# Cross-attention and a routed feed-forward on one core: turning activations through memory and VectorE's blocks instead of on TensorE, and writing the empty rows two at a time

## The chip, the cores and the metric

The kernel runs on one core of one Trainium2 chip. A core has TensorE (matmuls, in profiles PE, and its weight loads PEld), VectorE (DVE), ScalarE (ACT), GpSimd (POOL) and SyncE (SP), which run their own instruction streams and wait for each other through semaphores; 16 DMA engines move data between the device's memory, called DRAM in the code, and the core's SBUF. The metric is device time in microseconds for one execution. All data are 32-bit floats.

## The reference

Eight batches of 256 rows of 512 numbers are normalised, attend to a context, are added back, are normalised again, and go through a shared and a routed feed-forward layer.

```python
# x, ctx: (8, 256, 512)
def xattn(q, k, v):                      # 32 heads of 16, 8 groups of keys and values
    qh, kh, vh = heads(q @ Wq.T), heads(k @ Wk.T), heads(v @ Wv.T)
    attn = softmax(qh @ kh.T / sqrt(16))
    return (attn @ vh) @ Wfc.T + bfc

def ffn(h):                              # 8 experts, 352 wide; each row goes to 2
    scores = softmax(h @ gate_weight.T)  # 4 groups of 2; the 2 best groups count
    wmat = top2_within_best_groups(scores)
    routed = sum_n wmat[:, n] * ((silu(h @ gate_w[n].T) * (h @ up_w[n].T)) @ down_w[n].T)
    shared = (silu(h @ sh_gate_w.T) * (h @ sh_up_w.T)) @ sh_down_w.T   # 704 wide
    return routed + shared

x = x + xattn(layernorm(x), ctx, ctx)
x = x + ffn(layernorm(x))
```

## The kernel before

The contraction of a matmul runs over the 128 partitions, so an activation tile of 128 rows by 512 columns has to be turned before its columns can be contracted. The kernel does this in two places of the attention phase. In `project(b)` (L894) the normalised input rows of batch b are turned into `xT` and multiplied with `wq_sb` (L921). In `close(b)` (L1035), which multiplies the attention's result with `wfc_sb`, adds the residual into `acc` and normalises it, the normalised rows `lnf` are turned into `hT`; `hT` feeds the router's product (L1094) and the shared layer's first products (L181, `Shared.pieces`). Both use `transposed` (L822): four TensorE transposes of 128 x 128 into PSUM, and one copy into SBUF by ACT or VectorE, whichever `copy.free` names at that point. A batch has two row tiles (`q` or `qc`), so it takes two such calls in each place, in the profile `tx` and `th`.

The order of TensorE's, VectorE's, ACT's and SP's instructions is the order in which the program writes them down (L104). The main loop (L1386) goes through units of work: 64 times `maxima` (L948), the score products whose maximum VectorE takes (L964), and 64 times `weights` (L980), the same products turned, whose exponential ACT takes (L996). Both use the one PSUM tile `s`. Between them `Others.fill` (L300) puts pieces of other stages: `normed`, `keys`, `project`, `close`, `router`, `pieces`. Each stage is a generator; what it yields is the TensorE time that the piece is worth, and how much other work has to pass before its next piece may come (`rest`). `fill` fills a gap of about 2 to 3 us; if no stage is ready, and only in the first 44 steps, `warm` (L1275) puts in matmuls of the identity. `place` (L966) turns the maxima and sends them into `qT`; `values` (L1001) multiplies the exponentials with the values, and `divide` (L1017) divides on VectorE.

SP issues nearly all transfers, in program order: the loads of `x`, `acc` and the context, the eight pieces `qT<-q` and `kT<-k` of each batch that spread heads over bands of partitions, and the loads in `transfers` (L1367), one a step, of weights and of zeros.

In the last third each row sits in `rows`, a table in DRAM sorted by expert: each expert has its own region, into which `send` (L1172) scatters the rows. `routed` (L354) works through 8 + 24 + 3 tiles of 128 rows. `load(i)` (L396) brings a tile of rows with four transfers of 32 partitions, each partition taking 512-byte pieces, so that row i of a block of 32 lands in partition i of a quarter; `turn(i)` (L431) then transposes the 32 x 32 blocks on VectorE, which yields a turned tile whose contraction is dealt over groups of partitions, and the weights `wgu` are laid out to match (`up`, L1437). The weights of experts 1 and 2 are asked for before the loop, those of expert i + 3 at tile i, 1408 and 768 KB each. Behind the last row of every expert 64 rows of zeros, `blank`, have to stand, so that a partly filled tile adds nothing; where they go is known on the chip only, from `t_end`. The loop at L573 writes all eight, after the loads of tiles 0 to 2 and the weights 0 to 2. A transfer that reads `rows` waits for the writes before it, and a write for the reads before it. At tile n, `run` (L609) asks for tile n + 2's rows and then for expert n + 3's weights; `turn` of tile n + 1 stands before the products of tile n.

Of the kernel before, what the change touches and what calls it, by code (L numbers as in the profile page):

```python
# [43 lines left out]
F32 = mybir.dt.float32  # L44
# [40 lines left out]
@with_exitstack  # L85
def xattn_ffn(
    ctx: ExitStack,
    tc: tile.TileContext,
    x: bass.AP,
    ctxT: bass.AP,  # L90
    wq: bass.AP,
    wkv: bass.AP,
    wfc: bass.AP,
    bfc: bass.AP,
    wgate: bass.AP,
    wsg: bass.AP,
    wsd: bass.AP,
    wgu: bass.AP,
    wd: bass.AP,
    out: bass.AP,  # L100
):
    nc = tc.nc

    ctx.enter_context(tc.manual_schedule(engines={ENG.PE, ENG.Activation, ENG.DVE, ENG.SP}))  # L104

    keep = ctx.enter_context(tc.tile_pool(name="keep", bufs=1))
    dram = ctx.enter_context(tc.tile_pool(name="dram", bufs=1, space=bass.MemoryType.DRAM))
    ps_m = ctx.enter_context(tc.tile_pool(name="ps_m", bufs=3, space=PSUM))
    right = ctx.enter_context(ExitStack())
    left = ctx.enter_context(ExitStack())  # L110

    ident = keep.tile([P, P], F32, name="ident")
    make_identity(nc, ident)


    t_exp = keep.tile([P, N_PLAN], I32, name="t_exp")
    t_row = keep.tile([P, N_PLAN], I32, name="t_row")
    t_one = keep.tile([P, N_PLAN, N_EXP], F32, name="t_one")
    t_all = keep.tile([P, 1], I32, name="t_all")

    t_end = keep.tile([P, N_EXP], I32, name="t_end")

    blank = dram.tile([R, W], F32, name="blank")
    rows = dram.tile([N_EXP * S_R + P, W], F32, name="rows")


    kept = dram.tile([P, len(SCH), S], F32, name="kept")

    feed = Shared(right, tc, ps_m, wsg, wsd, out, kept)
    tail = attention(  # L130
        left, tc, ps_m, feed, x, ctxT, wq, wkv, wfc, bfc, wgate, out, ident,
        rows, t_exp, t_row, t_one, t_all, t_end, blank,
    )
    left.close()
    routed(
        ctx, tc, ps_m, wgu, wd, wsd, kept, ident,
        rows, t_exp, t_row, t_one, t_all, t_end, blank, out, tail, right,
    )


class Shared:
# [31 lines left out]
    def pieces(self, b):  # L173
        nc, ps_m = self.nc, self.ps_m
        hT = self.hT.pop(b)
        act = self.act
        for k, n in SCH:
            ps = ps_m.tile([P, 2, S], F32, tag="m", name=f"gu{b}_{k}")
            for i in range(2 if n == P else 1):
                for c in range(NC):  # L180
                    nc.tensor.matmul(  # L181
                        ps[:, i],
                        lhsT=self.gu[k][:, c, i * P : (i + 1) * P],
                        rhs=hT[:, c],
                        start=(c == 0),
                        stop=(c == NC - 1),
                    )
                    if c == 1 or (c == NC - 1 and i == 0 and n == P):
                        yield 0.88, True, 0
            gate, up = ps[:n, 0], ps[:, 1] if n == P else ps[n:, 0]  # L190

            sg = self.work.tile([P, S], F32, tag="sg", name=f"sg{b}_{k}")
            nc.scalar.activation(sg[:n], gate, AF.Tanh, scale=0.5)
            nc.vector.scalar_tensor_tensor(sg[:n], sg[:n], 1.0, gate, ALU.add, ALU.mult)
            nc.vector.scalar_tensor_tensor(act[:n, k], sg[:n], 0.5, up, ALU.mult, ALU.mult)
            yield 0.88, False, 0
        if b == B - 1:

            nc.sync.dma_start(self.kept, act)
            return  # L200
        acc = self.acc.pop(b)
        for q in range(QC):
            ps = ps_m.tile([P, D], F32, tag="m", name=f"o{b}_{q}")
            for i, (k, n) in enumerate(SCH):
                nc.tensor.matmul(  # L205
                    ps,
                    lhsT=act[:, k, q * P : (q + 1) * P],
                    rhs=self.down[:, k],
                    start=(i == 0),
                    stop=(i == len(SCH) - 1),  # L210
                )
                if i < len(SCH) - 1:
                    yield 0.88, True, 0
            nc.vector.tensor_add(acc[q], ps, acc[q])  # L214
            t0 = (b * QC + q) * P
            nc.sync.dma_start(self.out[t0 : t0 + P, :], acc[q])
            yield 0.88, False, 0
# [136 lines left out]
def routed(  # L354
# [215 lines left out]
        up_weights(e)  # L570
        down_weights(e)

    for e in range(N_EXP):  # L573
        to = value(t_end, e, ENG.SP, N_EXP * S_R)
        alone(tc, nc.sync.dma_start(rows[bass.ds(to, R), :], blank).ins)
    while tail.cost < tail.total - 2 * 0.88:
        tail.step()
    turn(0)
# [30 lines left out]
    def run(tiles):  # L609
# [3 lines left out]
        for n, i in enumerate(tiles):  # L613
            if 3 <= n + 2 < len(tiles):
                load(tiles[n + 2])
            if i + 3 < N_EXP:
                up_weights(i + 3)
                down_weights(i + 3)
            for k, at in zip(halfs, when):
                if at == n:  # L620
                    second(tiles[k])
            if n + 1 == len(tiles):
                last(i, tiles[n - 1])
                break
            if n == halfs[-1] + 2:
                down_sh, act_sh = two(len(SCH), D, len(SCH), S)
                nc.sync.dma_start(down_sh, wsd)
                nc.sync.dma_start(act_sh, kept)
            if n > 0:
                turn(tiles[n + 1])  # L630
            up(i)
            if n > 0:
                down(tiles[n - 1])
            else:
                turn(tiles[n + 1])
            turn_act(i)
# [27 lines left out]


def attention(
    ph, tc, ps_m, feed, x, ctxT, wq, wkv, wfc, bfc, wgate, out, ident,
    rows, t_exp, t_row, t_one, t_all, t_end, blank,
):

# [146 lines left out]
    def centred(dst, src, mv, rstd, q):  # L817
        nc.vector.tensor_scalar(
            dst, src, mv[:, q, 0:1], rstd[:, q : q + 1], ALU.subtract, ALU.mult
        )  # L820

    def transposed(row, dst, name):  # L822

        ps = ps_m.tile([P, NC, P], F32, tag="m", name=name)
        for c in range(NC):
            nc.tensor.transpose(ps[:, c], row[:, c * P : (c + 1) * P], ident)
        copy(dst, ps)

    copy = Copies(nc)
    qTs, os_, to_route = {}, {}, {}  # L830

    def normed(b):

        yield 0, False, 3.0 if b > 2 else 0, True
        xt = loaded[b]
        mv = small.tile([P, QC, 2], F32, tag="mva", name=f"mva{b}")
        for q in range(QC):
            moments(mv, xt[q], q, f"a{b}")
        rstd = deviation(mv, b, "a")
        yield 0, False, 2.0, True  # L840
        for q in range(QC):
            centred(xt[q], xt[q], mv, rstd, q)
        yield 0, False, 0, True

    put = {}
# [48 lines left out]
    def project(b):  # L894


        if b > 1:
            yield from keys(b)
        xt = loaded.pop(b)
        xT = p1.tile([P, NC, S], F32, tag="xT", name=f"xT{b}")  # L900
        for q in range(QC):
            transposed(xt[q], xT[:, :, q * P : (q + 1) * P], f"tx{b}_{q}")
            yield 0.44, False, 0.8 * q
        if b == 0:
            put[b](1, nc.scalar)

# [9 lines left out]
        for G in range(NG):  # L916
            ps = ps_m.tile([P, 2, S], F32, tag="m", name=f"pq{b}_{G}")
            for i in range(2):
                part = slice((2 * G + i) * P, (2 * G + i + 1) * P)
                for c in range(NC):  # L920
                    nc.tensor.matmul(  # L921
                        ps[:, i],
                        lhsT=wq_sb[:, c, part],
                        rhs=xT[:, c],
                        start=(c == 0),
                        stop=(c == NC - 1),
                    )
                    if c == 1 or (c == NC - 1 and i == 0):
                        yield 0.88, True, 0
# [105 lines left out]
    def close(b):  # L1035
# [28 lines left out]
        for qc in range(QC):  # L1064
            n = small.tile([P, W], F32, tag="row", bufs=4, name=f"lnf{b}_{qc}")
            centred(n[:, :D], acc[qc], mv, rstd, qc)
            n_rows.append(n)
        yield 0, False, 1.6
        hT = feed.hT[b] = feed.sums.tile([P, NC, S], F32, tag="hT", name=f"hT{b}")
        for qc, n in enumerate(n_rows):  # L1070
            transposed(n, hT[:, :, qc * P : (qc + 1) * P], f"th{b}_{qc}")
            yield 0.44, False, 1.0
        to_route[b] = hT, n_rows

    def ranks(s, n, name):
# [13 lines left out]
    def router(b, rest):  # L1089
# [2 lines left out]
        ps = ps_m.tile([P, S], F32, tag="m", name=f"lc{b}")  # L1092
        for c in range(NC):
            nc.tensor.matmul(  # L1094
                ps[32 * c : 32 * c + 32], lhsT=wg_sb[:, c], rhs=hT[:, c], start=True, stop=True
            )
        parts = small.tile([P, S], F32, tag="parts", bufs=1, name=f"parts{b}")
        copy(parts, ps)
# [168 lines left out]
        nc.vector.tensor_copy(t_row, row)  # L1267
        yield 0, False, 0.0

    PROJECT = 12 * 0.88 + 2 * 0.44  # L1270
    PROJECT_KEYS = 4 * 0.88
    CLOSE = 2 * (0.44 + 4 * 0.88)
    ROUTER = 0.6 + 0.45 + 0.45

    def warm():  # L1275
# [28 lines left out]
    of_keys = others.add(keys(1), PROJECT_KEYS, 0, 1)  # L1304
    for _ in range(2):
        others.step(of_keys)
    projected = [others.add(project(0), PROJECT - PROJECT_KEYS, 0, 1, norms[0])]
    others.finish(projected[0])
    gates = {}
    for b in range(1, B):  # L1310
# [1 line left out]
        projected.append(  # L1312
            others.add(
                project(b),
                PROJECT if b > 1 else PROJECT - PROJECT_KEYS,
                start,
                UNITS * b - 1.5 * LAG,
                projected[-1],
# [172 lines left out]
```

## Time and profile before

The median is 940.75 us over three runs (939.1 to 941.12). The profiled execution itself took 938.76 us.

| | us |
|---|---|
| profiled execution, on the device | 938.76 |
| its span, first to last instruction | 937.0 |
| TensorE busy | 910.8 |
| VectorE busy | 475.0 |
| ACT busy | 182.3 |
| GpSimd busy | 134.3 |

TensorE's granted clock is 0.993 of full over the execution. By stage, from windows of the profile (busy us of the engine in the window, and the DMA engines' mean busy share):

| window, us | TensorE | VectorE | ACT | DMA share | what runs |
|---|---|---|---|---|---|
| 13 to 100 | 86.51 | 46.70 | 22.28 | 0.58 | first projections, first units |
| 100 to 200 | 99.27 | 64.72 | 27.94 | 0.22 | units, shared layer of batch 0 |
| 200 to 400 | 197.67 | 127.77 | 57.02 | 0.12 | the same for later batches |
| 400 to 560 | 158.81 | 94.73 | 44.60 | 0.12 | the same |
| 586 to 634 | 47.88 | 26.32 | 5.60 | 0.34 | last router, plan, last shared products |
| 634 to 656 | 20.30 | 5.95 | 3.06 | 0.91 | routed tiles 0 to 2 |
| 656 to 668 | 0.92 | 1.62 | 0.00 | 1.03 | a wait for rows |
| 668 to 715 | 46.88 | 15.15 | 2.78 | 0.95 | routed tiles, weights still coming |
| 715 to 915 | 200.00 | 69.38 | 12.06 | 0.48 | routed tiles |

In a group of instructions, the page gives after the count the busy time and the mean duration of one in ns, then the engine's idle time just before them and what ended most of it. A 32-bit matmul appears as two passes, so the counts of L181 (704) are twice the program's (352); a transpose is one pass. A pass's duration includes the time in which the array drains, beside the next one, so the time that a stream of passes takes is read from the chain of waits or from starts.

### The profile page before, as it was taken

The numbers are of one execution on the slowest core, as the hardware profiler recorded it, in microseconds if no ns is written. First come the engines' busy times: TensorE is split into PE (matmuls) and PEld (weight loads), VectorE is DVE, ScalarE is ACT, GpSimd is POOL, SyncE is SP. The second block draws the span as 40 slices with busy tenths as digits, with TensorE's granted clock in tenths as the row PEclk, the third lists the DMA queues.
The fourth block names the chain that finished last, engine by engine and source line by source line (L and its number), as shares of the span: only waits on it lengthen the run. The fifth ranks groups of instructions, "written<-read, shape, count | busy, mean of one in ns | idle before, by whom it ended". The sixth has DMA issues, their size and how long they took to land.

```text
span 937.0 us, 13140 instructions
## 1 busy us (share of the span) xinstructions
PE 910.8 (97%) x4865; PEld 531.1 (57%) x4865; DVE 475.0 (51%) x1063; ACT 182.3 (19%) x222; POOL 134.3 (14%) x171
## 2 busy tenths in 40 slices
PE   9999999999999999999999999999599999999997
PEld 8775565536445554654654544775355555555553
DVE  4554867566755856654675655382233333333331
ACT  1224123223223222222222241101000000000000
POOL 4000100201101101010120121030012212121211
PEclk9999999999999999999999999999799999999999
DMA  6366620201102021011111011069995364644623
GB/s 223 86 180 220 192 46 2 82 6 35 48 13 81 24 46 47 1 53 35 36 48 35 13 48 57 12 219 294 347 341 105 69 164 71 157 78 87 149 38 75
DMA packets 59266, 90.45 MB, mean 97 GB/s; under 512 B 13312, under 2 KB 39680, under 8 KB 57152
## 3 DMA queue, kind: packets, MB, share of 16 engines
q1 hardware_dynamic: 50512, 70.63, 24.7%
q0 software_dynamic: 7648, 17.83, 9.4%
q10 hardware_dynamic: 1040, 1.12, 0.4%
q8 instruction: 41, 0.67, 0.3%
q14 instruction: 25, 0.20, 0.1%
HBM read 57.88 MB, written 27.24 MB: 91 GB/s over the span
## 4 chain that ended last, share of the span: by engine, by line
PE 89%; DVE 4%; DMA 3%; SPq 1%; issue 1%; ACT 1%; POOL 0%; ACTq 0%; DVEq 0%; POOLq 0%
PE rg L468 16%; PE gu L181 14%; PE ro L499 9%; PE o L205 8%; PE s L988 7%; PE s L955 7%; PE fc L1046 6%; PE pq L921 6%; PE av L1007 6%; PE pkv L865 2%; DVE nm L964 1%; PE pkv L854 1%; PE ra L491 1%; PE o L647 1%; PE tn L972 1%; PE warm L1279 1%
## 5 line engine op out<-in xcount | busy, mean ns | idle before, releaser
L964 DVE TENSOR_REDUCE nm<-s 128x8 f32<-128x2048 f32 x64 | 146.6, 2290 | 86.2 <-PE s L955 82.0
L468 PE MATMUL rg<-wgu_all,rxT 128*128 (+2 forms) x552 | 171.3, 464 | 1.1 <-DVE rxT L434 0.9
L181 PE MATMUL gu<-hT,gu_w 128*128 128x256 f32 x704 | 166.6, 385 | 0.0
L996 ACT ACTIVATE ex<-s 128x2048 f32<-128x2048 f32 x64 | 120.1, 1877 | 225.7 <-PE s L988 216.0
L181 PEld LDWEIGHTS gu<-hT,gu_w 128*128 128x128 f32 x704 | 129.1, 190 | 40.9 <-issue 24.6
L468 PEld LDWEIGHTS rg<-wgu_all,rxT 128*128 128x128 f32 (+1 forms) x552 | 100.6, 187 | 56.4 <-issue 8.8
L499 PE MATMUL ro<-wd_all,raT 128*128 (+5 forms) x210 | 96.5, 594 | 0.0
L513 POOL DMA_INDIRECT y<-ry,rid x38 | 58.4, 1537 | 239.5 <-DVE ry L510 156.0
L205 PE MATMUL o<-down,act 128*128 128x512 f32 x168 | 79.6, 604 | 0.3 <-DVE q L346 0.3
L988 PE MATMUL s<-qT,kT 17*128 17x512 f32 x512 | 73.0, 640 | 2.0 <-DVE nm L964 1.9
L955 PE MATMUL s<-kT,qT 16*128 16x256 f32 x1024 | 73.4, 400 | 1.5 <-ACT ex L996 0.8
L483 ACT ACTIVATE rsg<-rg 128x352 f32<-128x352 f32 x34 | 15.8, 464 | 253.2 <-PE rg L468 246.0
L955 PEld LDWEIGHTS s<-kT,qT 16*128 16x128 f32 x1024 | 46.3, 184 | 30.9 <-ACT ex L996 14.1
L499 PEld LDWEIGHTS ro<-wd_all,raT 128*128 128x128 f32 (+3 forms) x210 | 38.4, 186 | 42.9 <-issue 35.5
L921 PE MATMUL pq<-xT,wq_sb 128*128 128x256 f32 x256 | 61.2, 386 | 0.5 <-DVE acc L214 0.3
L1007 PE MATMUL av<-ex,v 128*32 128x512 f32 x512 | 61.5, 598 | 0.0
L1046 PE MATMUL fc<-wfc_sb,o 128*128 128x512 f32 x128 | 60.9, 604 | 0.1
L1173 POOL DMA_INDIRECT rows<-lnf,idx x32 | 31.7, 991 | 201.0 <-DVE idx L1167 190.2
L485 DVE TENSOR_TENSOR ract<-rg,rsg 128x352 f32<-128x352 f32 x34 | 17.8, 523 | 84.0 <-PE rg L468 84.0
L510 DVE TENSOR_SCALAR ry<-ro,rw 128x512 f32<-128x512 f32 x35 | 26.3, 750 | 66.7 <-PE ro L499 66.7
L921 PEld LDWEIGHTS pq<-xT,wq_sb 128*128 128x128 f32 x256 | 46.6, 190 | 14.5 <-issue 6.0
L205 PEld LDWEIGHTS o<-down,act 128*128 128x128 f32 x168 | 29.4, 190 | 35.8 <-issue 34.5
(184 smaller groups left out, 710.0 us busy)
## 6 DMA issues: line engine op xcount, KB each, us to landing
wgu_all<-wgu SPq DMA_DIRECT2D x8, 1408.0 KB
xs<-rows SPq DMA_DIRECT2D x128, 64.0 KB
wd_all<-wd SPq DMA_DIRECT2D x8, 768.0 KB
two<-wgu SPq DMA_DIRECT2D x3, 1408.0 KB
cT<-ctxT SPq DMA_DIRECT2D x8, 512.0 KB
acc<-x SPq DMA_DIRECT2D x16, 256.0 KB
y<-acc SPq DMA_DIRECT2D x16, 256.0 KB
x<-x SPq DMA_DIRECT2D x14, 256.0 KB
```

The lines of the kernel that those rows point to most:

```text
L181: nc.tensor.matmul(ps[:, i], lhsT=self.gu[k][:, c, i * P : (i + 1) * P], rhs=hT[:, c], start=(c == 0), stop=(c == NC - 1),)
L205: nc.tensor.matmul(ps, lhsT=act[:, k, q * P : (q + 1) * P], rhs=self.down[:, k], start=(i == 0), stop=(i == len(SCH) - 1),)
L468: nc.tensor.matmul(dst[part], lhsT=xTs[i][:, c, part.start // BAND : part.stop // BAND], rhs=w, start=(c == 0), stop=(c == NC - 1),)
L499: nc.tensor.matmul(o[part], lhsT=aTs[i][:fn, fc, part], rhs=w, start=(fc == 0), stop=(fc == len(FCH) - 1),)
L513: nc.gpsimd.indirect_dma_start(out=out, out_offset=bass.IndirectOffsetOnAxis(ap=to, axis=0), in_=y[part], in_offset=None, compute_op=ALU.add,)
L921: nc.tensor.matmul(ps[:, i], lhsT=wq_sb[:, c, part], rhs=xT[:, c], start=(c == 0), stop=(c == NC - 1),)
L955: nc.tensor.matmul(ps[:, r, j], lhsT=qT[band, G, j0 + j, qc * P : (qc + 1) * P], rhs=kT[band, G], start=True, stop=True,)
L964: nc.vector.tensor_reduce(nms[b, G, j0][:, qc], ps, AX.X, ALU.max, negate=True)
L988: nc.tensor.matmul(ps[:, r], lhsT=kT[band, G, kc * P : (kc + 1) * P], rhs=qT[band, G, j0 : j0 + 2], start=True, stop=True,)
L996: nc.scalar.activation(ex, ps, AF.Exp, scale=HD**-0.5)
L1007: nc.tensor.matmul(av[32 * r : 32 * r + 32], lhsT=vs[b % DEEP][:, kc, 4 * G + r], rhs=ex[:, r], start=(kc == 0), stop=(kc == QC - 1),)
L1046: nc.tensor.matmul(ps, lhsT=o[:, c, qc * P : (qc + 1) * P], rhs=wfc_sb[:, c], start=(c == 0), stop=(c == NC - 1),)
```

## The change

Inputs: for batches 2 to 7, `normed` writes the normalised rows to a DRAM scratch (`put_down`, two transfers of 256 KB); `project` reads them back at its start (`take_up`, four transfers of 64 KB, laid out as `load` does), and after the keys' products VectorE transposes the 32 x 32 blocks in place (`turn_blocks`, two instructions of 128 x 512). Batches 0 and 1 keep the TensorE transposes, with the columns regrouped while centring, so that the result has the same layout. Normalised sums: for batches 0 to 6 `close` does the same with `lnf`; batch 7 keeps TensorE, from a second centred copy. `xT` and `hT` become tiles of 8 blocks x 4 chunks x 32 columns, and the matmuls that read them take chunk c of all blocks, 8 runs of 32 columns. `wq`, `wgate` and the shared layer's first weights are laid out to match on the host (`banded`). The planner's sums of costs and some rests are set anew. Empty rows: instead of all eight before the loop, `run` writes two at each of tiles 0 to 3, after the rows of tile n + 2 and the weights of expert n + 3.

```diff
-                        rhs=hT[:, c],
+                        rhs=hT[:, :, c],
...
-    for e in range(N_EXP):
+    def empties(e):
+
         to = value(t_end, e, ENG.SP, N_EXP * S_R)
         alone(tc, nc.sync.dma_start(rows[bass.ds(to, R), :], blank).ins)
...
                 up_weights(i + 3)
                 down_weights(i + 3)
+            for e in range(N_EXP)[2 * n : 2 * n + 2]:
+                empties(e)
...
+    def by_chunks(row):
+
+        return row.rearrange("p (c k j) -> p k c j", c=NC, j=BAND)
+
+    def quarters(row):
+        return row.rearrange("p (k c j) -> p k c j", c=NC, j=BAND)
...
-        copy(dst, ps)
+        copy(dst.rearrange("p m c i -> p c m i"), ps.rearrange("p c (m i) -> p c m i", i=BAND))
+
+    def put_down(b, key, tiles):
+
+        where = dram.tile([S, D], F32, name=f"{key}{b}_rows")
+        for q, t in enumerate(tiles):
+            nc.sync.dma_start(where[q * P : (q + 1) * P, :], t[:, :D])
+        return where
+
+    def take_up(dst, where):
+        for r in range(NC):
+            nc.sync.dma_start(
+                dst[r * BAND : (r + 1) * BAND].rearrange("p m c i -> p m (c i)"),
+                where[:, r * P : (r + 1) * P].rearrange("(m i) d -> i m d", i=BAND),
+            )
+
+    def turn_blocks(t):
+        half = S // BAND // 2
+        for h in range(2):
+            part = t[:, h * half : (h + 1) * half].rearrange("p m c i -> p (m c i)")
+            nc.vector.transpose(part, part)
...
-        for q in range(QC):
-            centred(xt[q], xt[q], mv, rstd, q)
+        if b < 2:
+
+            xn = p2.tile([P, QC, D], F32, tag="o", name=f"xn{b}")
+            laid[b] = [xn[:, q] for q in range(QC)]
+            for q in range(QC):
+                centred(by_chunks(laid[b][q]), quarters(xt[q]), mv, rstd, q)
+        else:
+            for q in range(QC):
+                centred(xt[q], xt[q], mv, rstd, q)
+            laid[b] = put_down(b, "x", xt)
...
+        xT = p1.tile([P, S // BAND, NC, BAND], F32, tag="xT", name=f"xT{b}")
         if b > 1:
+            take_up(xT, laid[b])
             yield from keys(b)
...
-        for q in range(QC):
-            transposed(xt[q], xT[:, :, q * P : (q + 1) * P], f"tx{b}_{q}")
-            yield 0.44, False, 0.8 * q
+        del loaded[b]
+        if b < 2:
+            for q in range(QC):
+                transposed(laid[b][q], xT[:, q * NC : (q + 1) * NC], f"tx{b}_{q}")
+                yield 0.44, False, 0.8 * q
+        else:
+            yield 0, False, 1.0
+            turn_blocks(xT)
+            yield 0, False, 1.7
...
-                        rhs=xT[:, c],
+                        rhs=xT[:, :, c],
...
-        yield 0, False, 1.6
-        hT = feed.hT[b] = feed.sums.tile([P, NC, S], F32, tag="hT", name=f"hT{b}")
-        for qc, n in enumerate(n_rows):
-            transposed(n, hT[:, :, qc * P : (qc + 1) * P], f"th{b}_{qc}")
-            yield 0.44, False, 1.0
+        hT = feed.sums.tile([P, S // BAND, NC, BAND], F32, tag="hT", name=f"hT{b}")
+        feed.hT[b] = hT
+        if b < B - 1:
+            where = put_down(b, "h", n_rows)
+            yield 0, False, 3.0
+            take_up(hT, where)
+            yield 0, False, 4.0
+            turn_blocks(hT)
+            yield 0, False, 1.7
+        else:
+
+            for qc in range(QC):
+                n = p2.tile([P, D], F32, tag=f"x{qc}", bufs=1, name=f"hn{qc}")
+                centred(by_chunks(n), quarters(acc[qc]), mv, rstd, qc)
+                transposed(n, hT[:, qc * NC : (qc + 1) * NC], f"th{b}_{qc}")
+                yield 0.44, False, 1.0
...
-                ps[32 * c : 32 * c + 32], lhsT=wg_sb[:, c], rhs=hT[:, c], start=True, stop=True
+                ps[32 * c : 32 * c + 32], lhsT=wg_sb[:, c], rhs=hT[:, :, c], start=True, stop=True
...
-    PROJECT = 12 * 0.88 + 2 * 0.44
+    PROJECT = 12 * 0.88
     PROJECT_KEYS = 4 * 0.88
-    CLOSE = 2 * (0.44 + 4 * 0.88)
+    CLOSE = 2 * 4 * 0.88
...
-    projected = [others.add(project(0), PROJECT - PROJECT_KEYS, 0, 1, norms[0])]
+    projected = [others.add(project(0), PROJECT - PROJECT_KEYS + 0.88, 0, 1, norms[0])]
...
-                PROJECT if b > 1 else PROJECT - PROJECT_KEYS,
+                PROJECT if b > 1 else PROJECT - PROJECT_KEYS + 0.88,
...
+    def banded(w):
+
+        return w.T.reshape(NC, NC, BAND, -1).transpose(0, 2, 1, 3).reshape(P, NC, -1)
```

## The prediction

> **What bounds the kernel now.** I read the page first, then the table of windows, then the chain of waits and the timelines of the two stretches the change touches. The profiled execution took 938.76 us: the span and 1.76 us around it.
>
> ```profile
> span 937.0 us, 13140 instructions
> ...
> PE 910.8 (97%) x4865; PEld 531.1 (57%) x4865; DVE 475.0 (51%) x1063; ACT 182.3 (19%) x222; POOL 134.3 (14%) x171
> ...
> PE 89%; DVE 4%; DMA 3%; SPq 1%; issue 1%; ACT 1%; POOL 0%; ACTq 0%; DVEq 0%; POOLq 0%
> ...
> 100.00:200.00 100.00, 99.27 (x666) 56.60 (x665) 64.72 (x112) 27.94 (x32) 11.56 (x15) 1.00 0.22 60
> ...
> 656.00:668.00 12.00, 0.92 (x4) 0.33 (x3) 1.62 (x5) 0.00 (x0) 0.00 (x0) 0.74 1.03 361
> ```
>
> Columns of a window: length, busy time of PE, PEld, DVE, ACT, POOL, granted clock, DMA share, GB/s. TensorE is the bound from 13 us to 656 us (in the 100 us shown it is idle for 0.73), and its instructions go in program order, so TensorE time taken out counts, and each new wait in front of a matmul counts too. The exception is 656 to 668: DMA is saturated and TensorE idle.
>
> **What leaves TensorE.** Six of eight `tx` pairs and seven of eight `th` pairs go: 13 x 8 = 104 transposes. The chain has three such transposes in 0.33 us:
>
> ```profile
> 677.64 0.33 PE ra L491 x3
> ```
>
> So 104 x 0.11 = 11.4 us. But the planner decides what fills the room. The changed program, read in its order, has 62 `warm` matmuls where there were 34. Eight passes, that is four of these matmuls, take about 0.9 us net of drain, 0.22 each: 28 x 0.22 = 6.2 us come back. All of them lie before unit 44 of the order; there the new fill eats the whole saving (summing the matmuls ahead of it, unit 16's score product stands equally far in). Net on TensorE: **-5.2 us**, all of it in the later part.
>
> **What the round trip costs in the first 130 us.** A turned batch now needs two stores, four loads that wait for them, and two block transposes on VectorE. The nearest rows:
>
> ```profile
> 55.92 5.60 SPq L936 DMA_DIRECT2D qT<-q  x8
> 63.02 3.69 PE L921 MATMUL pq<-xT,wq_sb 128*128 128x256 f32 x16
> ...
> 655.80 2.15 SPq L407 DMA_DIRECT2D xs<-rows  x4
> ...
> 926.09 0.83 SPq L643 DMA_DIRECT2D sum<-y  x2
> ...
> 928.79 0.69 DVE L654 TENSOR_TENSOR sum<-o,sum 128x512 f32<-128x512 f32 x1 [7.92 <-DMA sum<-y]
> ...
> L434 DVE STREAM_TRANSPOSE rxT<-xs 128x512 f32<-128x512 f32 x35 | 24.5, 701 | 40.4 <-DMA xs<-rows 40.4
> ```
>
> Two 256 KB transfers are issued in 0.84 us, and the last of them lands 1.9 us later on a quiet queue (926.92 to 928.79). Four of the 64 KB loads take SP 1.8 us. Two block transposes are 1.4 us. No row shows SBUF going to memory and straight back; the Trainium skill (DMA: Bandwidth & Descriptors, "Anatomy of one DMA") says about 2.0 us fixed plus bytes at 436 GB/s for one transfer, 2.6 us for 256 KB, and calls memory the slowest target for the completion. By the row each landing is 1.9, by the page 2.6, which would add 0.7 to every trip; I take the row and keep the page for the range.
>
> Batch 3 is the worst. Its stores stand on SP behind the eight `qT` transfers of batch 2. From the end of the `q` copy (55.9): 5.6 + 0.84 + 1.9 + 1.8 + 1.9 + 1.4 = 13.4 us. TensorE reached the next projection 7.1 us after that copy (63.02); the new order takes 0.88 of `tx` out of this stretch and puts 1.32 of `warm` in, so 7.6. **Wait 5.8 us.** Batch 4 the same way: 7.1 for its `qT`, 1.5 for three stores of zeros, 7.8 as above, 16.4 in all; TensorE took 13.9 us from batch 3's last product (72.7) to the next projection (86.5), the new order adds 1.0, and the copy ends some 1.6 after the product: 13.3, so 3.1. Batch 2 has its stores long done: loads issued by 42.2, landed 44.1, turned 45.5, against 44.1 for TensorE: 1.4. Batch 5 is loaded in time, but its block transposes follow a 2.29 us maximum (L964) on VectorE: 0.1 + 2.3 + 1.4 = 3.9 after that score product, against 1.76 of fill: 2.2. For the first hT, VectorE does after its maximum (2.3) a division (1.8), statistics (1.9, then POOL's power 0.8), centring (1.0) and the turning (1.4): 9.3 against 6.2 of TensorE work: 3.2. Sum: **+15.7 us** (range 7 to 21). Behind each wait TensorE's whole queue stands.
>
> **Where the gaps lose their cover later.** The PSUM tile `s` has one buffer: after the first score product TensorE can't begin the next one until VectorE's maximum is done (2.29), and after the second until ACT's exponential is (1.88). From unit 44 on nothing fills a gap if no stage is ready. In the order of before, the one short gap is 0.8 us. In the new order four have nothing or little between: exponential 20 to maximum 25 (2.1) and on to exponential 21 (2.4); maximum 51 to exponential 47 (2.4, and 1.1 as an addition and the two turnings stand first on VectorE); exponential 54 to maximum 59 (1.2) and on to exponential 55 (2.4 + 1.1). With 0.5 at the third hT: 13.2 - 0.8 = **+12.4 us** (9 to 14). The other hT loads are ordered 6 to 9 us of TensorE work ahead of their turning, longer than the 3.7 us of issue and landing, so I cost them at nothing; without that cover each costs what it is late.
>
> **The routed stage.** Here DMA sets the time:
>
> ```profile
> 644.42 8.06 SPq L575 DMA_DIRECT2D rows<-blank  x8
> ...
> 655.80 2.15 SPq L407 DMA_DIRECT2D xs<-rows  x4
> ...
> 666.38 0.71 DVE L434 STREAM_TRANSPOSE rxT<-xs 128x512 f32<-128x512 f32 x1 [16.11 <-DMA xs<-rows]
> ...
> 667.68 0.90 PE L491 MATMUL ra<-ident,ract 128*128 128x128 f32 x3 [11.08 <-DVE ract L485]
> ```
>
> The rows of tile 3 are issued only when the eight blanks have landed, then stand behind `kept` and the weights of expert 3, and arrive at 666.4: TensorE is idle for 11.08 us. The change puts only two blanks before them, but now behind those weights, so the queue must run empty before the rows are even issued. Six blanks less, 0.6 us each at most (expert 2's 2.2 MB at 335 GB/s need 644.3 to 651, all eight had landed at 655.8), against a drained queue: tile 3 gains about 2 us. Then tiles 4, 5 and 6 each wait for two blanks of their own, which stand behind 2.2 MB of weights. A drain costs SP's 2.7 us from the blank's landing to the next weights and 1.2 of landing (the 1.9 without the transfer), less 0.8 for the rows that move in it and 0.6 of POOL's traffic: 2.5. With 1.2 for the blanks that is 3.7 per tile, 11 us. In before these tiles arrived every 8.05 us where TensorE needs 7.64, so there is no slack but about 1 us at tile 4. **+8 us** (2 to 12).
>
> **A rule that speaks against the change.** The Trainium skill (TensorE: Matmul & The Clock Gate, "The HAM clock gate") says an idle window of about 3.4 us halves the clock. The trace agrees after the 11.08 us: granted clock 0.50, then 0.67, and 16 passes took 6.48 instead of 4.74 us. For gaps of 4 to 6 us no row shows it. By the rule batch 3's wait costs 1.7 more, by the rows nothing; I take 0 and keep 1.7 for the range.
>
> **Other parts.** The matmuls that read xT and hT now take their 256 columns as eight runs of 32. No row has such an operand; contiguous passes take 0.23 us. The Trainium skill (SBUF — State Buffer, its note on 16-byte cachelines) charges only for leaving a line, and a run of 128 bytes stays in lines, so 0; the other end is 10 ns on each of 1024 passes, 10 us. Evacuations leave ACT and VectorE, block transposes come to VectorE: about +6 us there, hidden at 65% use but where named above.
>
> **Sum.** 938.8 - 5.2 + 15.7 + 12.4 + 8 = 969.7. The profiled run was 2 us below the median of 940.75; I forecast **969 us**.
>
> **Rivals.**
> B, the round trips are hidden: if the loads land before TensorE asks and only the gaps and the routed stage cost, 938.8 - 5.2 + 12.4 + 8 = 954. For it: SP may be freer than in before. Against: SP's eight `qT` alone fill 5.6 us.
> C, the operand in runs is slow: 980. For it: no row. Against: runs fill whole lines.
> D, **not slower**: the queue lets small transfers pass big ones. Then blanks and rows land some 3 us after issue, tile 3 is there before 657 us (the point from which this decides), and the 11.1 us of idleness and 1.7 of slow clock go; the early trips shrink to 6 and the gaps stay at 10: 938.8 - 5.2 - 12.8 + 6 + 10 = 937. Against: a 8 KB `mark` issued at 637.84 landed only at 644.28, behind expert 1's weights.
> That the transposes don't leave isn't open: the order shows 24 left of 128.
>
> **Chances.** Forecast 0.55, B 0.17, C 0.13, D 0.15. The range 946 to 988 takes in B and C and leaves D and the far tail out. Under 0.2% (about 2 us) nothing can be told apart here. Faster 0.12, same 0.03, slower 0.85; slower is all but D.
>
> **What would show it.** Right: waits of `pq` on VectorE's turning at batches 3 and 4, TensorE below 99% busy before 130 us, `nm` ending idle time near units 25, 51 and 59, and the turning of rows waiting on DMA at tiles 4 to 6. Wrong: the first 600 us at 99% busy, a `gu` pass above 0.23 us, or no idle stretch between expert 2 and expert 3.

## The result, and the profile after

The changed kernel takes 986.46 us (median of four runs, 984.75 to 990.65) against 940.93 us: a ratio of 1.049, 95% interval 1.045 to 1.053. It is slower by 45.5 us, where 28 us were forecast. The direction was right and the time lies inside the range, near its upper end. The profiled executions differ by 46.96 us (985.72 against 938.76), and what follows accounts for this difference.

The page of the changed kernel, with the lines that answer to those shown of before:

```profile
span 984.0 us, 13177 instructions
...
PE 922.7 (94%) x4817; PEld 535.2 (54%) x4817; DVE 480.4 (49%) x1069; ACT 179.1 (18%) x218; POOL 133.4 (14%) x171
...
PE 71%; DMA 9%; DVE 5%; SPq 2%; issue 1%; ACT 1%; POOL 0%; ACTq 0%; DVEq 0%; POOLq 0%
```

TensorE runs fewer passes (4817 for 4865) but is busy 11.9 us longer, so some passes must be slower. In the chain that ended last, DMA and VectorE now hold 14%, where they held 7%. The windows (length, busy time of PE, PEld, DVE, ACT, POOL, granted clock, DMA share, GB/s) tell where; the first line is of before, the others of after:

```profile
50.00:100.00 50.00, 49.77 (x350) 31.93 (x349) 26.70 (x47) 15.35 (x13) 1.38 (x2) 1.00 0.70 213
...
13.00:50.00 37.00, 33.87 (x236) 27.34 (x235) 18.92 (x23) 5.65 (x10) 1.40 (x2) 0.95 0.46 124
50.00:100.00 50.00, 43.44 (x289) 28.45 (x287) 20.41 (x33) 12.41 (x11) 1.38 (x2) 0.90 0.70 207
100.00:130.00 30.00, 25.25 (x155) 16.22 (x158) 18.80 (x25) 3.40 (x4) 3.37 (x3) 0.89 0.52 153
130.00:200.00 70.00, 64.53 (x446) 39.96 (x444) 41.66 (x84) 20.46 (x24) 3.93 (x8) 1.00 0.28 72
...
700.00:750.00 50.00, 39.47 (x118) 22.58 (x119) 12.50 (x35) 2.32 (x5) 6.79 (x5) 0.93 0.86 284
```

The granted clock of the changed kernel is below 1 in each of the first three. Before, it was 1.00 everywhere up to 656 us. The timeline of TensorE at the first waits (start, duration, passes, and in brackets the idle time before and what ended it):

```profile
46.63 5.20 PE L968 MATMUL pq<-xT,wq_sb 128*128 128x256 f32 x16 [3.07 <-DVE xT L860]
...
74.64 5.46 PE L968 MATMUL pq<-xT,wq_sb 128*128 128x256 f32 x12 [6.56 <-DVE xT L860]
...
105.32 6.57 PE L968 MATMUL pq<-xT,wq_sb 128*128 128x256 f32 x16 [2.92 <-DVE xT L860]
...
142.25 3.69 PE L968 MATMUL pq<-xT,wq_sb 128*128 128x256 f32 x16 [1.88 <-issue]
```

Sixteen passes of `pq` take 3.69 us at full clock (the last line, and the same row before the change). Behind waits of 3.07 and 2.92 us they take 5.20 and 6.57. Twelve behind the wait of 6.56 take 5.46, where twelve take 2.86 elsewhere. The windows directly behind the three waits show granted clocks of 0.71, 0.50 and 0.57. So these waits are paid twice: as idle time, and as a slow clock after it. The wait of 1.88 us is not.

The same happens later at the single-buffered score tile:

```profile
466.33 1.15 PE L1002 MATMUL s<-kT,qT 16*128 16x256 f32 x16
470.57 2.09 PE L1035 MATMUL s<-qT,kT 17*128 17x512 f32 x8 [3.09 <-DVE nm L1011]
...
473.11 1.08 PE L1152 MATMUL lc<-hT,wg_sb 128*32 128x256 f32 x8
474.12 4.81 PE L181 MATMUL gu<-hT,gu_w 128*128 128x256 f32 x16
```

Between the two score products TensorE has nothing to do until VectorE's maximum is taken. Behind that, a score product takes 2.09 instead of 1.14 us, eight `lc` passes 1.08 instead of 0.64 and sixteen `gu` passes 4.81 instead of 3.72.

The account, cut at the first product of the routed stage (at 635.07 us before, 673.78 us after):

| | us |
|---|---|
| idle gaps of TensorE over 0.3 us, from 13 us on: 36.3 for 4.7 | +31.6 |
| slow passes behind them, against the usual time of the same group: 7.0 early, 7.3 at three places at the score tile | +14.3 |
| the rest, which is transposes gone and identity matmuls come | -7.2 |
| **up to the routed stage** | **+38.7** |
| idle in the routed stage: 14.6 in five waits, for 11.1 in one | +3.5 |
| slow passes there, at more places than before, and a remainder | +4.8 |
| **routed stage** (310.2 for 301.9 from its first product to the end of the span) | **+8.3** |

### The profile page after: what moved, and what is told of

It is laid out like the page before. It is cut to its first block, busy times and chain, and to the rows that moved or that the text cites. A ratio compares the mean times of both kernels' runs of the same rounds, so it can differ in the third digit from the quotient of the medians.

```text
span 984.0 us, 13177 instructions
## 1 busy us (share of the span) xinstructions
PE 922.7 (94%) x4817; PEld 535.2 (54%) x4817; DVE 480.4 (49%) x1069; ACT 179.1 (18%) x218; POOL 133.4 (14%) x171
## 4 chain that ended last, share of the span: by engine, by line
PE 71%; DMA 9%; DVE 5%; SPq 2%; issue 1%; ACT 1%; POOL 0%; ACTq 0%; DVEq 0%; POOLq 0%
PE gu L181 14%; PE rg L468 13%; PE o L205 7%; PE ro L499 7%; PE s L1035 6%; PE fc L1093 6%; PE s L1002 6%; PE av L1054 5%; DMA rows<-blank 3%; PE pq L968 3%; DMA xs<-rows 2%; DVE nm L1011 2%; DMA y<-ry,rid 1%; PE ra L491 1%; PE tn L1019 1%
## 5 line engine op out<-in xcount | busy, mean ns | idle before, releaser
L468 PE MATMUL rg<-wgu_all,rxT 128*128 (+2 forms) x552 | 174.3, 470 | 2.8 <-DVE rxT L434 2.5
L181 PE MATMUL gu<-hT,gu_w 128*128 128x256 f32 x704 | 169.5, 390 | 0.0
L1035 PE MATMUL s<-qT,kT 17*128 17x512 f32 x512 | 75.8, 663 | 9.0 <-DVE nm L1011 8.3
L968 PE MATMUL pq<-xT,wq_sb 128*128 128x256 f32 x256 | 68.4, 421 | 14.4 <-DVE xT L860 12.5
L968 PEld LDWEIGHTS pq<-xT,wq_sb 128*128 128x128 f32 x256 | 52.5, 212 | 28.6 <-issue 17.2
L1231 POOL DMA_INDIRECT rows<-lnf,idx x32 | 31.6, 989 | 207.7 <-DVE idx L1225 156.0
L434 DVE STREAM_TRANSPOSE rxT<-xs 128x512 f32<-128x512 f32 x35 | 24.5, 701 | 54.4 <-DMA xs<-rows 54.4
```

The source lines that it names most:

```text
L181: nc.tensor.matmul(ps[:, i], lhsT=self.gu[k][:, c, i * P : (i + 1) * P], rhs=hT[:, :, c], start=(c == 0), stop=(c == NC - 1),)
L468: nc.tensor.matmul(dst[part], lhsT=xTs[i][:, c, part.start // BAND : part.stop // BAND], rhs=w, start=(c == 0), stop=(c == NC - 1),)
L968: nc.tensor.matmul(ps[:, i], lhsT=wq_sb[:, c, part], rhs=xT[:, :, c], start=(c == 0), stop=(c == NC - 1),)
L1035: nc.tensor.matmul(ps[:, r], lhsT=kT[band, G, kc * P : (kc + 1) * P], rhs=qT[band, G, j0 : j0 + 2], start=True, stop=True,)
```

## The experiments

**Does idle time lower the clock?** Identity matmuls are put ahead of the first products of batches 2 to 5, and the filling between score products may go on to the end.

```diff
-        dull = warm if i < 44 else None
+        dull = warm
...
             turn_blocks(xT)
             yield 0, False, 1.7
+            for _ in range({2: 6, 3: 14, 4: 6, 5: 3}.get(b, 0)):
+                warm()
```

> The changed kernel with matmuls of the identity put into TensorE's idle stretches: 12, 28, 12 and 6 more directly ahead of the first product of batches 2 to 5, and the filling between score products allowed to the end. No wait is taken away. Theory (idle time drops the clock, and what follows runs slower: 1.4 + 2.4 + 2.8 us after the three long waits of the first 110 us, some 6.5 us after three waits at the score tile): those 13 us go, 973 us, and the waits stay in length, now filled. Rival (the passes behind a wait are slow because they read a tile turned in place, in runs of 32): 986 to 988 us, the first 16 passes still 5 to 6.5 us.

970.32 us (969.74 to 973.68): 16.1 us faster than the change. The first products of batches 2, 3 and 4 in the timeline of this kernel, and last the score product whose place had the gap of 3.09 us:

```profile
47.19 3.69 PE L970 MATMUL pq<-xT,wq_sb 128*128 128x256 f32 x16 [0.48 <-issue]
...
65.08 8.30 PE L1339 MATMUL warm<-ident 128*128 128x128 f32 x72
76.12 4.15 PE L970 MATMUL pq<-xT,wq_sb 128*128 128x256 f32 x12 [2.73 <-DVE xT L860]
...
105.97 3.69 PE L970 MATMUL pq<-xT,wq_sb 128*128 128x256 f32 x16 [0.57 <-issue]
...
463.50 1.13 PE L181 MATMUL gu<-hT,gu_w 128*128 128x256 f32 x4
464.56 1.14 PE L1037 MATMUL s<-qT,kT 17*128 17x512 f32 x8
```

Batch 2's product begins at 47.19 instead of 46.63 and batch 4's at 105.97 instead of 105.32, so their waits are no shorter. But behind identity matmuls (28 passes of them ahead of batch 4) their sixteen passes are back at 3.69. They read the same operand in runs of 32, so the operand was not the cause; the idle time was. Batch 3's product begins at 76.12 instead of 74.64, behind a gap of 2.73 that stayed open, and its slowness goes in part (4.15 for 5.46).

The 16.1 us are not all the clock's. At 119 us this kernel is 2.8 us ahead of the change. That is less than the 7.0 us of slow passes there, because batch 3's product stays slow in part and all three begin later. The routed stage begins 14.6 us earlier (659.16), so some 12 us come between, and there the edit did more than fill. `fill` counts an identity matmul as work that has passed, which makes pieces of other stages ready sooner. Only 32 identity passes were put in behind 160 us, and in the place of the gap of 3.09 us stand `lc` and `gu` passes. So the gaps at the score tile (10.9 us) are closed, mostly by other work, and with them went the slow passes behind them (7.3). What the clock alone is worth there this run can't tell.

**Which part costs what?** Each of three runs undoes one part of the change.

```diff
# x_on_pe
-            take_up(xT, laid[b])
...
-            turn_blocks(xT)
...
+            transposed_plain(xt[q], xT[:, :, q * P : (q + 1) * P], f"tx{b}_{q}")
# h_on_pe
-            where = put_down(b, "h", n_rows)
-            take_up(hT, where)
-            turn_blocks(hT)
...
+            transposed_plain(n, hT[:, :, qc * P : (qc + 1) * P], f"th{b}_{qc}")
# blanks_front
-            for e in range(N_EXP)[2 * n : 2 * n + 2]:
-                empties(e)
...
+    for e in range(N_EXP):
+        empties(e)
```

> The changed kernel with the inputs turned on TensorE again (xT and wq as before), the normalised sums through memory, the blanks two at a time. Theory (waits for the round trips and the clock lost behind them): 14.4 us of waits ahead of the input products and 6.6 us of slow passes go, 48 transposes come back (5.3 us), some 26 identity matmuls go (5.7 us): -21 us, 965 us. Rival (the early loss has another cause, such as SP or VectorE being busier with the sums): not below 980 us.

961.46 us (959.15 to 963.18), 25.0 us less. The waits of `pq` are gone (0.2 us of idle time ahead of them), and no pass up to 130 us is slow.

> The changed kernel with the normalised sums turned on TensorE again (hT, wgate and the shared layer's weights as before), the inputs through memory, the blanks two at a time. Theory (what the sums cost is the cover of the gaps between score products): waits of 2.5 us for the first hT, 10.9 us at the score tile, 2.8 us for batch 7's second centring and 6.8 us of slow clock go, 56 transposes come back (6.2 us), some 10 identity matmuls go (2.2 us): -19 us, 967 us. Rival (the gaps come from the inputs' project stage being shorter, not from the sums): 980 us or more, with the waits of score products on the maximum still there.

967.12 us (966.45 to 967.83), 19.3 us less. The waits of TensorE in this kernel (in total, times, longest) beside those of the change:

```profile
PE pq L975 <- DVE xT L867: 11.1, 3, 5.1
PE s L1042 <- DVE nm L1018: 2.0, 4, 0.8
```

```profile
PE pq L968 <- DVE xT L860: 12.5, 3, 6.6
PE s L1035 <- DVE nm L1011: 8.3, 4, 3.1
PE s L1002 <- ACT ex L1043: 2.9, 2, 2.0
PE th L839 <- DVE hn L822: 2.8, 1, 2.8
```

Where the sums stay on TensorE, no wait at the score tile is above 1.5 us (at 122 us). Their transposes and the moment at which their products come were the cover; which of the two was not tried.

> The changed kernel with all eight blanks written ahead of the tiles' loop, as before. Theory: the routed stage took 8.3 us longer from its first product to the end; this goes, and one wait of 11 us for tile 3's rows takes the place of the five waits of 1.2 to 4.6 us: 978 us. Rival (weights and rows were late for the stage's own later start, or two at a time is the better order): 986 us or more.

976.4 us (974.34 to 976.53), 10.1 us less. Its routed stage is 299.5 us long, with the one long wait of before:

```profile
706.51 0.90 PE L491 MATMUL ra<-ident,ract 128*128 128x128 f32 x3 [10.12 <-DVE ract L485]
```

All three came within 4 us of the theory's number. The three savings add to 54.4 us, 8.9 more than the whole change costs, so the parts share cost. Which of it they share was not tried.

**Is it SP's queue that makes batch 3 late?** In one run GpSimd issues the stores and loads, in the other the `qT` transfers.

```diff
# pool_queue
-            nc.sync.dma_start(where[q * P : (q + 1) * P, :], t[:, :D])
+            nc.gpsimd.dma_start(where[q * P : (q + 1) * P, :], t[:, :D])
...
-            nc.sync.dma_start(
+            nc.gpsimd.dma_start(
# qT_pool
-    (nc.scalar if b == 0 and i else nc.sync).dma_start(
+    (nc.scalar if b == 0 and i else nc.sync if b == 0 else nc.gpsimd).dma_start(
```

> The changed kernel with the stores and loads of the round trips issued by GpSimd instead of SyncE; blanks as changed. Theory (batch 3's and 4's stores stood behind eight qT transfers of 5.2 us on SP): the waits ahead of the first input products fall from 3.1, 6.6 and 2.9 us to at most 2.5 each, and their slow passes go for the most part: 973 us. Rival (the trip's own landings set the wait, or GpSimd issues more slowly): waits as long or longer, 986 us or more.

989.74 us (983.16 to 994.79), not to be told from the change (984.75 to 990.65). SP's queue and VectorE in the changed kernel, and then GpSimd's issues and VectorE in this one, at batch 3:

```profile
60.08 5.20 SPq L983 DMA_DIRECT2D qT<-q  x8
65.38 1.00 SPq L846 DMA_DIRECT2D x_rows<-x  x2
68.71 1.80 SPq L851 DMA_DIRECT2D xT<-x_rows  x4
...
73.23 1.31 DVE L860 STREAM_TRANSPOSE xT<-xT 128x512 f32<-128x512 f32 x2 [7.38 <-DMA xT<-x_rows]
```

```profile
59.96 1.16 POOL L846 DMA_DIRECT2D x_rows<-x  x2 [0.88 <-DVE x L822]
65.41 2.35 POOL L851 DMA_DIRECT2D xT<-x_rows  x4 [4.29 <-PE warm L1337]
...
73.76 1.30 DVE L860 STREAM_TRANSPOSE xT<-xT 128x512 f32<-128x512 f32 x2 [9.60 <-DMA xT<-x_rows]
```

The stores start 5.4 us earlier, yet the turning begins half a microsecond later: from the end of the stores' issue to the loads is 4.3 us instead of 2.3, and from the end of the loads' issue to the turning 6.0 instead of 2.7. Batch 2's wait of 3.07 us disappeared, and batch 3's grew from 6.56 to 9.27: TensorE came earlier to the same moment.

> The changed kernel with the eight qT transfers of batches 1 to 7 issued by GpSimd, so that on SyncE nothing stands ahead of the stores. Theory (batch 3's trip is late because its stores and loads queue behind 5.2 us of qT issues): the loads are issued by 66 instead of 70.5 us, the wait of 6.6 us ahead of batch 3's input products falls to 2 to 3, batch 4's 2.9 to 0, their slow passes go: 977 us. Rival (as with the stores and loads on GpSimd, the transfers take longer by what they start earlier, since the DMA engines are busy with weights and inputs): the waits stay within 1 us, 984 us or more.

983.93 us (977.32 to 986.69), so the total can hardly be told from the change either; the trace can. The wait at batch 3 is 5.15 us, at batch 4 0.92. The loads are issued by 65.9 us and the turning begins at 68.34, 4.9 us earlier, but the centring ended 2.7 us earlier too (58.65 for 61.34). From there to the turning it takes 9.7 us instead of 11.9. So of the 5.2 us that SP spends on `qT`, 2.2 show in the trip. Most of the rest is lost again: the loads come 4.1 us after the stores' issue instead of 2.3, and their own issue takes 2.8 us instead of 1.8. Whether that is contention with the weights and inputs that are loaded at this time (DMA share 0.70 from 50 to 100 us) was not separated.

**What can the empty rows be worth?** Tiles 0 to 7 are the first 128 rows of each expert, which are filled with zeros at the start; only later tiles read a blank. So the blanks can go behind the rows of tile 7.

```diff
# blanks_late_before, and the same on the change: blanks_late_after
-    for e in range(N_EXP):
-        to = value(t_end, e, ENG.SP, N_EXP * S_R)
+    def empties(e):
+        to = value(t_end, e, ENG.SP, N_EXP * S_R)
...
                 down_weights(i + 3)
+            if n == N_EXP - 3:
+                for e in range(N_EXP):
+                    empties(e)
```

> The kernel before, with one thing changed: the eight blanks are written after the rows of tile 7 have been asked for (tiles 0 to 7 are the first 128 rows of each expert, which were filled with zeros at the start, so only later tiles need the blanks), at a time when no weights are left in the queue. Theory (rows are late because the writes of blanks are waited for in a full queue): the 11.1 us wait for tile 3's rows shrinks to about 2, the slow clock behind it (2 us) goes: 930 us. Rival (the DMA engines are saturated by weights anyway, so tile 3's rows and weights can't come earlier): at least 8 us of the wait stay, 938 us or more.

948.62 us, a ratio of 1.0099 (1.0077 to 1.0121) to before: slower, which neither theory had. The wait at tile 3 fell as forecast, if less far, and another came at tile 8:

```profile
662.53 0.90 PE L491 MATMUL ra<-ident,ract 128*128 128x128 f32 x3 [5.10 <-DVE ract L485]
714.10 0.90 PE L491 MATMUL ra<-ident,ract 128*128 128x128 f32 x3 [10.60 <-DVE ract L485]
```

SP waits until 692.73 for tile 7's rows to land, then issues eight blanks in 7.96 us, then 2.2 MB of another expert's weights, and only then tile 8's rows.

> The changed kernel with all blanks after the rows of tile 7. Theory: the five waits of 1.2 to 4.6 us for rows (14.6 us) shrink to about 2 and 2.6 us of slow clock more than before's go: 970 us. Rival (the weights' bytes set the stage): 980 us or more.

988.97 us, the same miss: waits of 4.63 us at tile 3 and 10.51 at tile 8.

Four more runs move what stands around the blanks, each on the kernel before and with the blanks behind tile 7's rows as above:

```diff
# blanks_late_quick
+        to = value(t_end, e, ENG.Pool if e % 2 else ENG.SP, N_EXP * S_R)
+        q = nc.gpsimd if e % 2 else nc.sync
-        when = [N_EXP - 3, *(n + 3 for n in halfs)]
+        when = [N_EXP - 2, *(n + 3 for n in halfs)]
# weights_split: this, and
                 load(tiles[n + 2])
+                if n + 2 < N_EXP:
+                    down_weights(n + 2)
...
-                down_weights(i + 3)
# load7_early: this, and
-                load(tiles[n + 2])
+                if n + 2 != N_EXP - 1:
+                    load(tiles[n + 2])
+                if n + 2 == N_EXP - 2:
+                    load(tiles[n + 3])
# load7_sync: load7_early with all blanks on nc.sync
```

> The kernel before with the eight blanks after the rows of tile 7, four of them issued by SyncE and four by GpSimd, and the next expert's second pair of weights (2.2 MB) asked for one tile later, behind tile 8's rows. With all blanks on SyncE and the weights ahead of the rows, tile 3's wait was 5.1 us instead of 11.1, but tile 8's rows brought a new wait of 10.6 us. Theory (that wait is eight issues of 1 us and 2.2 MB ahead of the rows): it falls to at most 2 us, 936 us. Rival (the landing of the blanks itself is what tile 8 waits for): 5 us or more stay, 942 us.

> The same, and the rows of tiles 3 to 7 stand between the two weights of their expert instead of behind both. Theory (rows queue behind the bytes ahead of them): tile 3's rows come about 2 us earlier, 0.79 MB at 360 GB/s, if the second weight is not late in its place: 934 us. Rival (the wait of 5.1 us is the bytes of the whole stage, in whatever order): no difference to the run beside it.

> The kernel before with blanks, second weights and weight order as in the run weights_split, and tile 7's rows asked for right behind tile 6's, ahead of 2.2 MB of weights of expert 7 and the second part of expert 6's. In weights_split the blanks waited for tile 7's rows until 692.2 us, and tile 8's rows then came 4.7 us late. Theory (the blanks wait for rows that stand behind weights): the blanks are issued by about 685 us and land behind the last weights, tile 8's wait and the slow passes behind it (4.7 and 1.7 us) go, 932 us. Rival (the last weights keep the queue full until 692 us, so the blanks land no earlier): 938 us.

> As the run load7_early, but all eight blanks on SyncE. There SyncE issued its four by 687.2 us, while GpSimd's four began only at 693.4 us, behind the addition of a tile's results on its own queue, and tile 8's wait stayed at 4.3 us. Theory (the late blanks were GpSimd's): SyncE issues all eight by 692 us, tile 8's rows come before 700 us, its wait and slow passes (some 6 us) go, 932 us. Rival (the blanks land late whatever issues them, behind the last weights): the wait stays above 3 us, 937 us.

| run | us | ratio to before | TensorE waits at tiles 3, 8, 9 | first product to tile 9 |
|---|---|---|---|---|
| before | 940.93 | | 11.08, 0, 0 | 88.6 |
| blanks_late_quick | 940.16 | 0.9994 (0.9981 to 1.0007) | 5.47, 1.99, 0.94 | 88.8 |
| weights_split | 938.28 | 0.9973 (0.9960 to 0.9986) | 3.73, 4.70, 0.53 | 88.5 |
| load7_early | 937.83 | 0.9977 (0.9961 to 0.9994) | 3.17, 4.25, 0 | 88.1 |
| load7_sync | 938.77 | 0.9972 (0.9956 to 0.9988) | 4.11, 1.43, 2.91 | 88.1 |

The last column is the time from the first routed product to the turning of tile 9's activations. A wait at tile n is one for its rows; it shows at `ract`, the activations of the tile before, because the turning of tile n stands ahead of them on VectorE. Each order shortens the wait it aims at, and a later tile pays. In the profiles the stage up to tile 9 is at most 0.6 us shorter than before. In load7_early the blanks that GpSimd issued came at 693.4 us, behind an addition of results on its own queue. With all on SP they were issued by 694.2, and tile 9's rows then stood behind 2.2 MB of weights:

```profile
684.92 9.32 SPq L575 DMA_DIRECT2D rows<-blank  x8
696.78 1.94 SPq L407 DMA_DIRECT2D xs<-rows  x4
...
700.09 0.35 SPq L428 DMA_DIRECT2D two<-wgu  x1
...
701.71 2.00 SPq L407 DMA_DIRECT2D xs<-rows  x4
```

The theory's 932 to 936 us were missed in all four. The rival, that the bytes of the stage set its time in any order, is not shown either: from 680 to 690 us the DMA share is 0.71 in load7_sync, so there is some room (it is 1.01 in the 15 us ahead of that). Asking for the second weights still later was not tried, and what bounds this stage stays open. What stands is small: three of these versions beat the kernel before by 0.23 to 0.28%, and where most of that comes from was not found.

## Why the prediction was right, and where it was off

**The early trips** were forecast at 1.4, 5.8, 3.1, 2.2 and 3.2 us (15.7 in all). They are 3.07, 6.56, 2.92, 1.88 and 2.46: 16.9. The working held, with two slips. The four loads of a trip are 128 KB each, not 64 as the texts above have it; their issue takes 1.80 us all the same. And batch 3's two landings took 2.3 us (stores) and 2.7 (loads), nearer to the 2.6 that was kept for the range than to the 1.9 that was taken, although the Trainium skill's figure (DMA: Bandwidth & Descriptors, "Anatomy of one DMA") is fitted to transfers that GpSimd issues, and these are SyncE's. In two of the five places the views name another releaser (`issue`, `qT<-q`), but VectorE's turning ends 0.1 and 0.2 us before the product begins. That the stores stand behind `qT` was right as an order and too simple as a price, as the two GpSimd runs show.

**The gaps at the score tile** came at the forecast places. They are 2.00 and 2.41 (exponential 20, maximum 25, exponential 21), 3.09 (maximum 51 to exponential 47), 0.94 and 2.42 (exponential 54, maximum 59, exponential 55): 10.9, where 13.2 was forecast. Waits that the forecast didn't name made up for it: 2.76 for batch 7's second centring `hn`, 1.08 for the router's `sel`, and 1.6 more at the first routed tile. In all the idle time up to the routed stage grew by 31.6 us, where 28.1 was forecast.

**TensorE's own work** fell by 7.2 us (a difference, not counted), where 5.2 was forecast.

**The routed stage** was forecast at +8 and is +8.3. The rows of tiles 4, 5 and 6 arrive 11.45, 11.95 and 12.31 us after those of the tile before, where 8.05 + 3.7 was forecast. SP's waits for the blanks, in the view of its queue for 640 to 760 us before and after, are the drained queue of the forecast:

```profile
SPq L407 <- DMA rows<-blank: 1.4, 1, 1.4
...
SPq L407 <- DMA rows<-blank: 29.2, 4, 10.8
```

The agreement of the sum is partly luck: tile 3 gained 4.8 us and not 2 (turned 26.5 us after the first product for 31.3), and the slow passes, which the forecast left out, took it back.

**The term that failed** is the rule that the prediction weighed and set aside. It read: "By the rule batch 3's wait costs 1.7 more, by the rows nothing; I take 0". Slow passes cost 14.3 us before the routed stage alone, most of the 16.1 us by which the step sum (+30.9) fell short of the profiled difference (+47.0). The one row of before that showed it, 16 passes in 6.48 us behind an idle stretch of 11 us, was read as a matter of long stretches. That the time still lies inside the range is partly luck: the range gave the clock 1.7 us, and part of its room at the top was meant for rival C, which did not come. The Trainium skill (TensorE: Matmul & The Clock Gate, "The HAM clock gate") gives about 3.4 us of idleness. This kernel's clock fell at less: by the rule as it stands only batch 3's wait would have been charged, and the measurement charges six places before the routed stage.

**The rivals.** B fell with the waits of `pq`: the trips were not hidden. C fell with the shared layer's products: twelve `gu` passes take 2.86 us in both kernels and sixteen `pq` passes 3.69, so an operand in eight runs of 32 costs nothing here. D fell with SP's waits for the blanks, 29.2 us for 1.4.

## What to carry to other kernels

Price a new wait on a full engine twice, as idle time and as what the clock does behind it; on this kernel the second was 14 us for 32 us of the first. Work that looks like waste on the busiest engine can be what covers another engine's latency: taking the sums' 56 transposes away (about 6 us by the 0.11 of the prediction) uncovered three places where nothing else was ready. A small write that must land before the next read can cost what stands ahead of it in the queue, and in every order tried here moving it passed the wait on to a later reader.

## What the runs showed that was not expected

The clock's threshold is not one length of idle time. In the changed kernel single gaps of 1.88, 2.46 and 2.76 us left the granted clock at 1.00. Gaps of 2.92, 3.07 and 3.09 lowered it, and so did pairs of short ones: 2.00 and 2.41 us with one score product of 1.15 us between them, and 0.94 and 2.42. In the run x_on_pe single gaps of 2.06 and even 1.41 us were enough (clock 0.50 and 0.59 behind them). And the same gap at the same place can do either: behind 1.88 us batch 5's sixteen passes took 3.69 us in the changed kernel, and in pool_queue

```profile
142.13 5.38 PE L968 MATMUL pq<-xT,wq_sb 128*128 128x256 f32 x16 [1.88 <-issue]
```

The gap of 2.76 us ahead of `hn` left the clock at 1.00 in the changed kernel, and 0.58 stood behind it in warm_gaps. So no length of a single gap, from 1.4 to 2.8 us, decides it here. The fall can come inside the gap; the windows of the changed kernel around its gap of 3.09 us, and then those of x_on_pe around that of 2.06:

```profile
467.50:470.50 3.00, 0.00 (x0) 0.00 (x0) 3.00 (x3) 0.00 (x0) 0.08 (x1) 0.84 0.68 193
470.50:475.00 4.50, 4.43 (x20) 1.60 (x21) 0.44 (x2) 2.12 (x2) 2.44 (x2) 0.50 0.13 48
```

```profile
133.20:135.30 2.10, 0.06 (x4) 0.09 (x8) 1.83 (x4) 1.88 (x1) 0.00 (x0) 0.92 0.54 83
135.30:137.00 1.70, 1.70 (x10) 0.80 (x11) 0.42 (x1) 0.00 (x0) 0.00 (x0) 0.50 0.00 0
```

What counts beside the length was not tried. The Trainium skill (TensorE: Matmul & The Clock Gate, "The HAM clock gate") says that the gate looks at a window of about 3.4 us that runs freely. That the same gap does either could come from where it falls in such a window; but a gap shorter than the window can't leave it wholly idle, so the page's rule alone would charge none of these.

The filling of gaps reached further than its purpose: 74 more identity matmuls, whose results nobody reads (272 passes of `warm` for 124), went with 16 us less, partly for the clock and partly because the program's planner, which counts them as work, then placed other pieces where the gaps had been.
